# One transposed copy of the tokens, router logits as extra columns, and a gather on ScalarE, in a block of two attentions and a mixture of experts

## The chip, the cores and the metric

The kernel runs on one core of one Trainium2 chip. The metric is the device time of one execution in microseconds. A core has five engines that work beside each other, each with its own in-order queue: TensorE (PE in the profile, its weight loads are PEld), VectorE (DVE), ScalarE (ACT), GpSimd (POOL) and SyncE (SP), whose queue issues most of the DMAs. An engine that has to wait for another one waits on a semaphore, and everything behind that instruction in its queue waits with it. TensorE writes into PSUM, eight banks of 2 KB per partition; here they form two pools of four, `pu` (called by `bank_u`) and `pw` (`bank_w`).

## The reference

Everything is float32. The input `x` has 32 sequences of 256 positions with 128 features. What is computed, cut to what matters:

```
xn  = (x - mean) / sqrt(var + 1e-5)                     # over the 128 features
out = x + attn(xn) + ffn(xn)

attn(x):  q, k, v = x@Wq, x@Wk, x@Wv                    # 16 heads of 8, over the 256 positions
          scores = centred q . centred k / 8 + var(q) var(k) / 8
          return softmax(scores) @ v @ Wo

ffn(x):   hn  = layernorm(x, ln1_w, ln1_b)
          qkv = hn @ in_proj_w.T + in_proj_b            # causal attention over the first axis, 16 heads of 8:
          x1  = x + attention(qkv) @ out_proj_w.T + out_proj_b     # the 32 sequences at one position
          hn2 = layernorm(x1, ln2_w, ln2_b)
          logits = hn2 @ router_w.T                     # 8 experts, the best 2 of their softmax
          y = sum over the 2 of gate * gelu(hn2 @ w1[e]) @ w2[e]
          return x1 + y
```

So there are two attentions over the same normalised input. The one in `ffn` runs along the first axis: its "sequence" is the 32 sequences at one of the 256 positions.

## The kernel before

The 8192 tokens are handled twice, in two orders.

**The first stage** is the attention of `ffn`. It works in 16 chunks of 16 positions x 32 sequences, which makes 512 tokens, or 4 tiles of 128. `first_rounds` is a software pipeline written out by hand: iteration `i` takes chunk `i+5` from memory (`load`), measures chunk `i+4` (`measure`, by `stats`: mean and variance on DVE, the powers on POOL), normalises chunk `i+3` on ACT (`norms`), transposes and projects chunk `i+2` (`turn_in`, `project_in`), makes the scores of chunk `i+1` (`scores`, then `lessened`, which takes the row maximum off, on DVE, and `exponents` on ACT), applies the weights of chunk `i` (`turn_weights`, `weigh`, `divide`) and closes chunk `i-1` (`turn_out`, `project_out`, `normalise`). Two more steps belong to chunk `i-2`: `turn_normed` and `logits`. The order of the calls in the loop of `first_rounds` (L465 to L527) is the order in which instructions stand in each engine's queue.

For each chunk `turn_in` (L303) makes two transposed forms. One is of the normalised tokens, kept for the second stage in `xnT` (L305). The other is of the tokens normalised a second time (`zn`, L295); ScalarE applies `ln1_w` and `ln1_b` to it while it copies it out as `hT` (L310). `project_in` (L313) multiplies `hT` by the three projections: `pk` (L316), copied out by ACT in four masked forms `kb` (L320, four instructions), `pq` (L322), copied out as `qT` (L324), and `pv` (L327), copied out as `v` (L328). `v` goes to memory and back in another arrangement (`vald`, `spread`). `project_out` (L419) makes `px` (L424), adds the tokens on DVE (L426) and measures the sum; `normalise` (L433) writes the second layernorm without weights on POOL into `zx` (L436); `turn_normed` (L440) transposes that and applies `ln2_w`, `ln2_b` (L442); `logits` (L445) multiplies it by the router (L448) and DVE copies the result to `lg` (L449).

**The second stage** is the other attention, the routing and the experts. It counts in steps `t` of two heads (`step`, L942); four even values of `t` make one unit `u`, one half of the heads of a sequence, and there are 64 units. Each step has the score matmuls `sm` (L610) and `sT` (L616), the maxima on DVE (L622) and the exponentials on ACT (L625). In a step with `x == 2` comes `project` (L555): one matmul over 128 tokens of one sequence, whose stationary operand is `xnT` read with a stride of 32 elements (L557), then a square (L563) and a copy (L565) on ACT; `project_rest` (L568) copies the values out, one half on ACT (L573), one on DVE (L576). In `x == 4` comes `turn_qk` (L578), whose `pqk` is copied out by ACT (L589, L591) and DVE (L592). The steps `t = -14 .. -2` run beside what is left of the first stage (`last_rounds`).

From `t = 0` on, `route` (L717) is mixed in, some calls per step (`some`, L992: four per unit up to `t = 96`, then eight). It picks the two experts of each token, counts places, writes places and gates to memory and reads them in the order of the sequences (L792 to L798), and scatters the tokens by 128 indirect DMAs of POOL (L801). At `t = 256` the experts run as one block, and then the other 32 units with the gathers of the experts' results.

Of the kernel before, what the change touches and what calls it, by code (L numbers as in the profile page):

```python
# [19 lines left out]
P = 128  # L20
# [48 lines left out]
def block_kernel(  # L69
# [26 lines left out]
    xv = x.rearrange("s (i c k) e -> i c s (k e)", c=4, k=4)  # L96
# [7 lines left out]
    xnT = cp.tile([P, NCHUNK, 512], F32, name="xnT")  # L104
# [14 lines left out]
    rv = resd.rearrange("s (i c k) e -> i c s (k e)", c=4, k=4)  # L119

    vec = cp.tile([P, 7], F32, name="vec")
    l1w, l1b, l2w, l2b = (vec[:, n:n + 1] for n in range(4))
# [5 lines left out]
    mhalf = cp.tile([P, 4, 1], F32, name="mhalf")  # L128
    wqkv = cp.tile([P, 3, P], F32, name="wqkv")
    wo = cp.tile([P, P], F32, name="wo")  # L130
    inT = cp.tile([P, 3, P], F32, name="inT")
    outT = cp.tile([P, P], F32, name="outT")
    rT = cp.tile([P, NE], F32, name="rT")

# [5 lines left out]
    def load(i):  # L140
        xt = ax.tile([P, 4, P], F32, tag="xt", name=f"xt{i}")
        for c in range(4):
            nc.sync.dma_start(xt[32 * c:32 * c + 32].rearrange("s k e -> s (k e)"), xv[i, c])
        return xt
# [13 lines left out]
    late = xnT[:, NCHUNK - 2:NCHUNK].rearrange("p i t -> p (i t)").rearrange("p (n m) -> p n m", m=P)  # L158
    ipw, opw, qkw, rw, bvs = late[:, 0:3], late[:, 3], late[:, 4:6], late[0:NE, 6], late[:, 7]
    qkT, ccen = zx[:, NTILE - 2:NTILE], zx[:, NTILE - 3]  # L160

    def loads():

        xts[0] = load(0)
        for n, v in enumerate((ln1_w, ln1_b, ln2_w, ln2_b)):
            nc.scalar.dma_start(vec[:, n:n + 1], v.rearrange("(p o) -> p o", o=1))
        nc.scalar.dma_start(vec[:, 4:7], in_proj_b.rearrange("(t p) -> p t", p=P))
        nc.sync.dma_start(cst, consts[:, 0:C_CEN])
        nc.sync.dma_start(ipw, in_proj_w.rearrange("(t p) e -> p t e", p=P))
        nc.scalar.dma_start(opw, out_proj_w)  # L170
        nc.scalar.dma_start(bout, out_proj_b.partition_broadcast(P))
        xts[1] = load(1)
        nc.sync.dma_start(qkw[:, 0, :], Wq)
        nc.sync.dma_start(qkw[:, 1, :], Wk)
        nc.sync.dma_start(rw, router_w)
        xts[2] = load(2)
        nc.sync.dma_start(ccen, consts[:, C_CEN:C_ALL])
        nc.sync.dma_start(wqkv[:, 2, :], Wv)
        nc.sync.dma_start(wo, Wo)

    def set_in():
        nc.vector.tensor_scalar(bk4, cst[:, C_M4:C_M4 + 4], bk, None, ALU.mult)
        pt = bank_u([P, 4, P], "pt0")
        for n in range(3):
            nc.tensor.transpose(pt[:, n, :], ipw[:, n, :], ident)
        nc.tensor.transpose(pt[:, 3, :], opw, ident)
        nc.vector.tensor_copy(inT[:, 0:2, :], pt[:, 0:2, :])

        nc.vector.tensor_copy(
            inT[:, 2, :].rearrange("p (j g d) -> p j g d", j=4, g=4),  # L190
            pt[:, 2, :].rearrange("p (g j d) -> p j g d", j=4, g=4),
        )
        nc.vector.tensor_copy(outT, pt[:, 3, :])


        nc.vector.tensor_copy(bvs, bv.to_broadcast([P, P]))
        pbo = bank_u([P, P], "pbo")
        nc.tensor.matmul(pbo, bvs, outT, start=True, stop=True)
        nc.vector.tensor_tensor(bout, bout, pbo, ALU.add)

    def set_rest():
        pt = bank_w([P, 4, P], "pt1")
        nc.tensor.transpose(pt[:, 0, :], qkw[:, 0, :], ident)
        nc.tensor.transpose(pt[:, 1, :], qkw[:, 1, :], ident)
        nc.tensor.transpose(pt[:, 2, 0:NE], rw, ident[0:NE, 0:NE])
        nc.vector.tensor_copy(qkT, pt[:, 0:2, :])
        nc.vector.tensor_copy(rT, pt[:, 2, 0:NE])
        pb = bank_w([P, 2, P], "pqkw")
        for n in range(2):
            nc.tensor.matmul(pb[:, n, :], qkT[:, n, :], ccen, start=True, stop=True)  # L210
        nc.vector.tensor_copy(wqkv[:, 0:2, :], pb)

# [29 lines left out]

    def set_values(n):
        nc.gpsimd.memset(vs[n].rearrange("p j k g d -> p (j k g) d")[:, :, HD:HD + 1], 1.0)
        nc.gpsimd.memset(vbs[n], 0.0)
# [9 lines left out]
    xts, rss, nrm, mvs, zns, hTs, qTs, kbt, scs, prs, pTs, wps, os, oTs, x1s, h2s = ({} for _ in range(16))  # L255

    def stats(src, tag, i, bufs=2):

        st = a2.tile([P, 4, 6], F32, tag="st", name=f"st{tag}{i}")
        mv = a2.tile([P, 4, 2], F32, tag=f"mv{tag}", name=f"mv{tag}{i}")  # L260
# [3 lines left out]
        rs = a2.tile([P, 4, 1], F32, tag=f"rs{tag}", name=f"rs{tag}{i}")  # L264
# [4 lines left out]
    def measure(i):  # L269
# [10 lines left out]
        nc.gpsimd.tensor_tensor(r2, r2, mhalf, ALU.pow)  # L280
        nrm[i] = rs, nb, r2

# [20 lines left out]
    def turn_in(i):  # L303

        nc.scalar.copy(  # L305
            xnT[:, i, :].rearrange("p (c k s) -> p k c s", c=4, k=4),
            transposed(tokens(i), "a", i).rearrange("p (k c s) -> p k c s", k=4, c=4),
        )
        hTs[i] = a2.tile([P, 512], F32, tag="hT", name=f"hT{i}")
        nc.scalar.activation(hTs[i], transposed(zns.pop(i), "b", i), AF.Identity, bias=l1b, scale=l1w)  # L310
        nc.gpsimd.tensor_tensor(tokens(i), tokens(i), bout.unsqueeze(1).to_broadcast([P, 4, P]), ALU.add)

    def project_in(i):  # L313
        hT = hTs.pop(i)
        pk = bank_w([P, 512], f"pk{i}")
        nc.tensor.matmul(pk, inT[:, 1, :], hT, start=True, stop=True)  # L316
# [5 lines left out]
        nc.tensor.matmul(pq, inT[:, 0, :], hT, start=True, stop=True)  # L322
        qTs[i] = a2.tile([P, 512], F32, tag="qT", name=f"qT{i}")
        nc.scalar.activation(qTs[i], pq, AF.Identity, bias=bq, scale=1.0)  # L324
        pv = bank_u([P, 4, 4, 32], f"pv{i}")
        for k in range(4):
            nc.tensor.matmul(pv[:, :, k, :], hT[:, k * P:(k + 1) * P], inT[:, 2, :], start=True, stop=True)  # L327
        nc.scalar.copy(  # L328
            vs[i % 2].rearrange("p j k g d -> p (j k g) d")[:, :, 0:HD],
            pv.rearrange("p j k (g d) -> p (j k g) d", d=HD),  # L330
        )
        nc.sync.dma_start(vald[i], vs[i % 2].rearrange("p j k g d -> p j (k g d)"))
# [86 lines left out]
    def project_out(i):  # L419

        oT = oTs.pop(i)
        px = bank_w([P, 4, P], f"px{i}")
        for k in range(4):
            nc.tensor.matmul(px[:, k, :], oT[:, k * P:(k + 1) * P], outT, start=True, stop=True)  # L424
        x1 = x1s[i] = a2.tile([P, 4, P], F32, tag="x1", name=f"x1{i}")
        nc.vector.tensor_tensor(x1, px, tokens(i), ALU.add)  # L426
# [3 lines left out]
        for c in range(4):  # L430
            nc.sync.dma_start(rv[i, c], xt[32 * c:32 * c + 32].rearrange("s k e -> s (k e)"))

    def normalise(i, eng=nc.gpsimd):  # L433
        x1, mv, rs = x1s.pop(i), mvs.pop(i), rss.pop(i)
        for k in range(4):
# [4 lines left out]
    def turn_normed(i):  # L440
        h2s[i] = a2.tile([P, 512], F32, tag="h2", name=f"h2{i}")
        nc.scalar.activation(h2s[i], transposed(tokens(i), "c", i), AF.Identity, bias=l2b, scale=l2w)  # L442

    def logits(i):
        pl = bank_u([P, 4, NE], f"pl{i}")  # L445
        h2 = h2s.pop(i)
        for k in range(4):
            nc.tensor.matmul(pl[:, k, :], h2[:, k * P:(k + 1) * P], rT, start=True, stop=True)  # L448
        nc.vector.tensor_copy(lg[:, 4 * i:4 * i + 4, :], pl)  # L449
# [4 lines left out]
    def first_rounds():  # L454
# [7 lines left out]
        measure(1)  # L462
        set_values(0)
        for i in range(-2, NCHUNK):
# [23 lines left out]
            if i == NCHUNK - 1:  # L488
                project(0, 0)
                project_rest(0, 0)  # L490
# [5 lines left out]
            if i == -2:  # L496
                set_rest()
                set_values(1)
                nc.gpsimd.memset(zero, 0.0)
            if 3 <= i < 3 + NV:  # L500
                set_second(i - 3)
            if chunk(i + 3):
                norms(i + 3)
            if chunk(i + 4):
# [4 lines left out]
            if chunk(i - 1):  # L509
                normalise(i - 1)  # L510
            if chunk(i + 1):
                scores(i + 1)
            if chunk(i - 2):
                turn_normed(i - 2)
# [10 lines left out]
            if chunk(i - 2):  # L525
                logits(i - 2)

    def last_rounds():
# [5 lines left out]
        yield turn_normed(n - 1)  # L534
        yield project_out(n)
        yield logits(n - 1)
        yield normalise(n, nc.vector)
        yield turn_normed(n)
        yield logits(n)
# [5 lines left out]
    xs_all = xnT.rearrange("p i (b s) -> p (i b) s", s=NB)  # L545
    NU = 2 * NB
    pps = {}
    ot, qas, kas, exs, pos, oas, res = {}, {}, {}, {}, {}, {}, {}
# [5 lines left out]
    def project(s, ti):  # L554
# [3 lines left out]
            pp.rearrange("p n m -> p (n m)"), xs_all[:, ti * P:(ti + 1) * P, s],  # L558
# [4 lines left out]
        nc.scalar.activation(sq, pqk, AF.Square, scale=1.0 / math.sqrt(HD - 1))  # L563
        qk = qkts[s % NQ][:, ti].rearrange("p n g m r -> p (n g m) r")
        nc.scalar.copy(qk[:, :, 0:HD], pqk)  # L565
        pps[s, ti] = pp, sq

    def project_rest(s, ti):  # L568
# [4 lines left out]
        nc.scalar.copy(vo[:, :, 0, 0:8], pi[:, :, 0])  # L573
        qk = qkts[s % NQ][:, ti].rearrange("p n g m r -> p (n g m) r")
        nc.vector.tensor_reduce(qk[:, :, HD:HD + 1], sq, AX.X, ALU.add)
        nc.vector.tensor_copy(vo[:, :, 1, 8:16], pi[:, :, 1])  # L576
# [140 lines left out]
    def route():  # L717
# [3 lines left out]
        oh1, oh2 = r_tile("oh1", NTILE, NE), r_tile("oh2", NTILE, NE)  # L721
        yield nc.vector.tensor_reduce(m, lg, AX.X, ALU.max)
# [69 lines left out]
        for name, dram, src, dt in (("posb", posd, posi, I32), ("gateb", gated, gates, F32)):  # L792
            dv = dram.rearrange("s (i c k) u -> c s i (k u)", c=4, k=4)
            for c in range(4):
                nc.sync.dma_start(dv[c], src[32 * c:32 * c + 32].rearrange("p (i k) u -> p i (k u)", k=4))
# [146 lines left out]
    def step(t):  # L942
# [21 lines left out]
        if x == 6 and 0 <= u < NU:  # L964
            weigh_head(u, 0)
# [55 lines left out]
```

## Time and profile before

| what | value |
|---|---|
| median of 3 runs | 989.93 us (988.33 to 993.07) |
| the profiled execution, its own time | 992.8 us |
| its span in the trace | 991.0 us |
| mean granted TensorE clock | 0.976 |
| busy over the span | PE 940.2, DVE 706.3, ACT 655.1, POOL 561.9 us |

By stretch, busy microseconds of each engine:

| stretch, us | what runs | length | PE | DVE | ACT | POOL | clock |
|---|---|---|---|---|---|---|---|
| 0 to 60 | start, first chunks | 60 | 40.47 | 24.98 | 35.62 | 30.98 | 0.91 |
| 60 to 280 | the chunks | 220 | 197.62 | 151.12 | 158.63 | 153.74 | 0.93 |
| 280 to 300 | into the second stage | 20 | 17.63 | 17.78 | 9.08 | 2.35 | 0.83 |
| 300 to 565 | 32 units, routing, scatter | 265 | 265.00 | 231.33 | 179.96 | 124.38 | 1.00 |
| 565 to 715 | experts | 150 | 148.20 | 65.82 | 89.15 | 48.24 | 1.00 |
| 715 to 991 | 32 units, gathers, results | 276 | 271.30 | 215.29 | 182.71 | 202.23 | 1.00 |

Busy time of matmuls is modelled and they are pipelined, so a PE that is "busy" all the time need not be at its peak. The first instruction of the routing (L722) starts at 290.65 us; the first matmul of the experts that reads scattered tokens starts at 569.82 us.

### The profile page before, as it was taken

To read this page: it belongs to the slowest core of one execution; us is meant where nothing else is said; L and a number is where in the kernel's file an instruction comes from. 1 tells how busy PE (TensorE), PEld (TensorE's weight loads), DVE (VectorE), ACT (ScalarE), POOL (GpSimd) and SP (SyncE) were. 2 spreads that over 40 slices of the span, in tenths; PEclk is the share of its full clock that TensorE was granted. 3 is DMA by queue.
4 is the path that set the end of the run, shared out by engine and by line. 5 is a ranking of instruction groups with operands and counts; after the bars stand their busy time and mean duration, and the time that the engine had idled before them with its cause. 6 is when DMAs were issued, how large, how long until landed. Compare 5 with 4: busy or idle time off the path is not lost.

```text
span 991.0 us, 32300 instructions
## 1 busy us (share of the span) xinstructions
PE 940.2 (95%) x13107; PEld 679.0 (69%) x13107; DVE 706.3 (71%) x1638; ACT 655.1 (66%) x1362; POOL 561.9 (57%) x725
## 2 busy tenths in 40 slices
PE   4788999989789999999999999999999999999998
PEld 2567777777666666666666689999866666666664
DVE  2477578667589999888888834444588888888882
ACT  4687878877446666666666665555666666676664
POOL 5468787785310002777777123333387888888870
PEclk9798999999889999999999999999999999999999
DMA  3344434422031000541111134444222321121220
GB/s 100 108 132 125 134 120 139 140 60 68 21 102 35 2 2 15 59 111 55 55 53 54 52 117 135 133 134 136 76 60 63 81 69 36 39 68 52 55 60 22
DMA packets 87747, 76.32 MB, mean 77 GB/s; under 512 B 32840, under 2 KB 70864, under 8 KB 87600
## 3 DMA queue, kind: packets, MB, share of 16 engines
q1 hardware_dynamic: 74736, 48.03, 17.4%
q0 software_dynamic: 11600, 26.10, 8.5%
q8 instruction: 103, 1.69, 0.7%
q10 hardware_dynamic: 1264, 0.14, 0.1%
q14 instruction: 44, 0.36, 0.1%
HBM read 33.98 MB, written 40.24 MB: 75 GB/s over the span
## 4 chain that ended last, share of the span: by engine, by line
PE 86%; DVE 7%; issue 2%; POOL 2%; ACT 1%; DMA 0%; ACTq 0%; DVEq 0%; SPq 0%; POOLq 0%
PE sm L610 26%; PE pav L634 13%; PE pe L854 6%; PE pp L557 6%; PE ph L845 6%; PE pqk L584 3%; PE ptp L300 2%; PE sT L616 2%; PE pt L653 2%; PE sc L359 2%; DVE pr L375 2%; PE px L834 2%; PE pk L316 2%; PE px L424 2%; PE py L687 2%
## 5 line engine op out<-in xcount | busy, mean ns | idle before, releaser
L625 ACT ACTIVATE ex<-sT 128x512 f32<-128x512 f32 x512 | 277.7, 595 | 179.0 <-PE sT L616 179.0
L622 DVE TENSOR_REDUCE mt<-sm 128x2 f32<-128x512 f32 x512 | 329.0, 686 | 73.6 <-PE sT L616 67.7
L610 PE MATMUL sm<-ka,qa 32*128 32x256 f32 x2048 | 292.4, 402 | 3.5 <-DVE mt L622 3.5
L616 PE MATMUL sT<-qa,ka 32*128 32x256 f32 x2048 | 291.0, 400 | 0.0
L610 PEld LDWEIGHTS sm<-ka,qa 32*128 32x128 f32 x2048 | 177.4, 185 | 81.0 <-issue 38.1
L616 PEld LDWEIGHTS sT<-qa,ka 32*128 32x128 f32 x2048 | 176.4, 184 | 2.6 <-issue 1.7
L801 POOL DMA_INDIRECT xsd<-zx,posi x128 | 122.9, 960 | 81.4 <-DVE posi L789 42.7
L905 POOL DMA_INDIRECT yg<-ysd,posb x128 | 122.1, 954 | 43.0 <-issue 31.5
L634 PE MATMUL pav<-ex,va 128*32 128x256 f32 x2048 | 137.2, 385 | 0.0
L859 POOL DMA_DIRECT2D ysd<-ye x71 | 48.2, 679 | 115.0 <-DVE ye L858 89.1
L634 PEld LDWEIGHTS pav<-ex,va 128*32 128x32 f32 x2048 | 53.8, 109 | 64.2 <-issue 24.0
L854 PEld LDWEIGHTS pe<-w,ge 128*128 128x128 f32 x568 | 74.5, 192 | 4.2 <-ACT ge L847 0.7
L854 PE MATMUL pe<-w,ge 128*128 128x128 f32 x568 | 74.9, 275 | 0.3 <-ACT ge L847 0.3
L845 PE MATMUL ph<-xT,w 128*128 128x256 f32 x284 | 73.3, 381 | 0.0
L557 PE MATMUL pp<-wqkv,xnT 128*128 128x384 f32 x128 | 65.6, 595 | 0.8 <-DVE mt L622 0.8
L858 DVE COPY ye<-pe 128x256 f32<-128x256 f32 x71 | 30.1, 424 | 50.8 <-PE pe L854 50.8
L837 ACT ACTIVATE xT<-px,vec 128x256 f32<-128x256 f32 x71 | 39.9, 563 | 35.8 <-PE px L834 35.8
L847 ACT ACTIVATE ge<-ph 128x512 f32<-128x512 f32 x71 | 42.4, 597 | 21.1 <-PE ph L845 21.1
L378 ACT ACTIVATE pr<-pr 128x1024 f32<-128x1024 f32 x32 | 33.8, 1058 | 34.0 <-DVE pr L375 33.9
L374 DVE TENSOR_REDUCE mx<-sc 128x16 f32<-128x512 f32 x64 | 43.4, 678 | 17.3 <-PE sc L359 17.3
L828 DVE COPY w<-wall 128x512 f32 x71 | 30.4, 429 | 33.3 <-issue 31.9
L845 PEld LDWEIGHTS ph<-xT,w 128*128 128x128 f32 x284 | 48.5, 191 | 4.1 <-ACT xT L837 0.4
(170 smaller groups left out, 1663.0 us busy)
## 6 DMA issues: line engine op xcount, KB each, us to landing
xb<-xsd SPq DMA_DIRECT2D x71, 128.0 KB, 2.1
ysd<-ye POOLq DMA_DIRECT2D x71, 128.0 KB
xsd<-zero SPq DMA_DIRECT2D x10, 852.0 KB
vald<-v SPq DMA_DIRECT2D x16, 288.0 KB, 2.3
vb<-vald SPq DMA_DIRECT2D x64, 72.0 KB, 3.0
xt<-in_L_attn_x_dram SPq DMA_DIRECT2D x64, 64.0 KB, 2.0
resd<-xt SPq DMA_DIRECT2D x64, 64.0 KB, 1.7
res<-resd SPq DMA_DIRECT2D x32, 128.0 KB, 3.3
```

Source lines behind the costliest of these rows:

```text
L374: nc.vector.tensor_reduce(mx, s, AX.X, ALU.max)
L557: nc.tensor.matmul(pp.rearrange("p n m -> p (n m)"), xs_all[:, ti * P:(ti + 1) * P, s], wqkv.rearrange("p n m -> p (n m)"), start=True, st ...
L610: nc.tensor.matmul(sc[:, i, :], qas[u][r:r + 32, i * P:(i + 1) * P], kas[u][r:r + 32, h, :], start=True, stop=True,)
L616: nc.tensor.matmul(sc[:, i, :], kas[u][r:r + 32, h, i * P:(i + 1) * P], qas[u][r:r + 32, :], start=True, stop=True,)
L622: nc.vector.tensor_reduce(mts[y // 8 % 2][:, :, o:o + 1], sc, AX.X, ALU.max, negate=True)
L625: nc.scalar.activation(exs[y], sc, AF.Exp, scale=1.0 / HD)
L634: nc.tensor.matmul(pos[u][32 * j:32 * j + 32, :], vaugs[s % NV][:, ti, 4 * j + 2 * g + h, :], exs[8 * u + 4 * h + j][:, ti, :], start=(h = ...
L801: yield nc.gpsimd.indirect_dma_start(xsd_views[n * NTILE + k], bass.IndirectOffsetOnAxis(ap=posi[:, k, n:n + 1], axis=0), zx[:, k, :], None,)
L845: nc.tensor.matmul(ph[:, f, :], wb[n][0][:, f * P:(f + 1) * P], xT, start=True, stop=True)
L854: nc.tensor.matmul(pe[:, j, :], ge[:, f, j * P:(j + 1) * P], w2b[:, f, :], start=(f == 0), stop=(f == 1))
L859: nc.gpsimd.dma_start(ysd[n * BLK:(n + 1) * BLK].rearrange("(p j) h -> p j h", j=2), ye)
L905: yield nc.gpsimd.indirect_dma_start(yg[s][:, ti, n, :], None, ysd, bass.IndirectOffsetOnAxis(ap=gt["posb"][:, s, ti, n:n + 1], axis=0),)
```

## The change

What it does, part by part:

- **One transposed form.** `turn_in` transposes only `zn`; the copy goes to `znT`, which takes the place of `xnT` and is kept for the second stage. `ln1_w` is folded into the projections (`inT`, `inV`), `ln1_b` into their biases (`set_in`). The order of tokens in a chunk changes from (c, k) to (k, c), so that the rows of `x` are read, and those of `resd` written, in pieces of 128 elements and no longer of 512.
- **The second stage reads `znT`**, which was scaled a second time, and takes that scaling back: `invert` keeps the reciprocals in `rall`, `scale_back` brings them through memory into the order of the sequences (`rpos`), and `project` and `project_rest` multiply by them. `gather` copies the 256 columns of one sequence out of `znT` into a contiguous tile on ScalarE; `project` reads that.
- **Extra columns for the logits.** `turn_normed` and `logits` are gone. The logits are built from the values' matmul, which has 160 columns instead of 128 and is made in two halves, and from the output's matmul, 136 columns instead of 128, also in halves; a multiplication, two additions and, in `route`, five POOL instructions over 64 x 8 elements put them together.
- **Filling and measuring moved.** `measure(1)` stands between the weights' copies in `set_in`; `set_values(1)` and the zero tile are filled one iteration later. Of the four instructions of `normalise`, two move from POOL to DVE.

```diff
-    xv = x.rearrange("s (i c k) e -> i c s (k e)", c=4, k=4)
+    xv = x.rearrange("s (i k c) e -> i c s k e", c=4, k=4)
...
     def set_in():
-        nc.vector.tensor_scalar(bk4, cst[:, C_M4:C_M4 + 4], bk, None, ALU.mult)
...
-        nc.vector.tensor_copy(inT[:, 0:2, :], pt[:, 0:2, :])
...
+        nc.tensor.transpose(pr, rw, ident[0:NE, 0:NE])
+        nc.vector.tensor_scalar(inT, pt[:, 0:2, :], l1w, None, ALU.mult)
+        measure(1)
+
+        nc.vector.memset(inV[:, 4, :], 0.0)
+        nc.vector.tensor_scalar(
+            inV[:, 0:4, :].rearrange("p j (g d) -> p j g d", g=4),
             pt[:, 2, :].rearrange("p (g j d) -> p j g d", j=4, g=4),
+            l1w, None, ALU.mult,
         )
+        nc.vector.tensor_copy(rT, pr)
+        nc.vector.tensor_scalar(rP, rT, l2w, None, ALU.mult)
+        nc.vector.tensor_tensor(ipb, ipw, l1bs.unsqueeze(1).to_broadcast([P, 3, P]), ALU.mult)
+        nc.vector.tensor_reduce(bz, ipb, AX.X, ALU.add)
+        nc.vector.tensor_tensor(vec[:, 4:7], vec[:, 4:7], bz.rearrange("p n o -> p (n o)"), ALU.add)
+        nc.vector.tensor_scalar(bk4, cst[:, C_M4:C_M4 + 4], bk, None, ALU.mult)
         nc.vector.tensor_copy(outT, pt[:, 3, :])
...
+    def invert(i):
+
+        nc.vector.reciprocal(rall[:, 4 * i:4 * i + 4], r2s.pop(i).rearrange("p k o -> p (k o)"))
...
     def turn_in(i):
-
-        nc.scalar.copy(
-            xnT[:, i, :].rearrange("p (c k s) -> p k c s", c=4, k=4),
-            transposed(tokens(i), "a", i).rearrange("p (k c s) -> p k c s", k=4, c=4),
-        )
-        hTs[i] = a2.tile([P, 512], F32, tag="hT", name=f"hT{i}")
-        nc.scalar.activation(hTs[i], transposed(zns.pop(i), "b", i), AF.Identity, bias=l1b, scale=l1w)
+        nc.scalar.copy(znT[:, i, :], transposed(zns.pop(i), "b", i))
         nc.gpsimd.tensor_tensor(tokens(i), tokens(i), bout.unsqueeze(1).to_broadcast([P, 4, P]), ALU.add)
...
-        pv = bank_u([P, 4, 4, 32], f"pv{i}")
-        for k in range(4):
-            nc.tensor.matmul(pv[:, :, k, :], hT[:, k * P:(k + 1) * P], inT[:, 2, :], start=True, stop=True)
-        nc.scalar.copy(
-            vs[i % 2].rearrange("p j k g d -> p (j k g) d")[:, :, 0:HD],
-            pv.rearrange("p j k (g d) -> p (j k g) d", d=HD),
-        )
-        nc.sync.dma_start(vald[i], vs[i % 2].rearrange("p j k g d -> p j (k g d)"))
+
+        v = vs[i % 2]
+        for h in range(2):
+            pv = bank_u([P, 5, 2, 32], f"pv{i}_{h}")
+            for k in range(2):
+                o = (2 * h + k) * P
+                nc.tensor.matmul(pv[:, :, k, :], zT[:, o:o + P], inV, start=True, stop=True)
+            nc.scalar.copy(
+                v[:, :, 2 * h:2 * h + 2].rearrange("p j k g d -> p j (k g) d")[:, :, :, 0:HD],
+                pv[:, 0:4].rearrange("p j k (g d) -> p j (k g) d", d=HD),
+            )
+            t = slice(4 * i + 2 * h, 4 * i + 2 * h + 2)
+            nc.vector.tensor_tensor(
+                lg[:, t, :], pv[:, 4, :, 0:NE], rall[:, t].unsqueeze(2).to_broadcast([P, 2, NE]), ALU.mult
+            )
+        nc.sync.dma_start(vald[i], v.rearrange("p j k g d -> p j (k g d)"))
...
     def project_out(i):
...
-        nc.vector.tensor_tensor(x1, px, tokens(i), ALU.add)
+        for h in range(2):
+            px = bank_w([P, 2, P + NE], f"px{i}_{h}")
+            for k in range(2):
+                o = (2 * h + k) * P
+                nc.tensor.matmul(px[:, k, :], oT[:, o:o + P], outX, start=True, stop=True)
+            nc.vector.tensor_tensor(
+                x1[:, 2 * h:2 * h + 2, :], px[:, :, 0:P], tokens(i)[:, 2 * h:2 * h + 2, :], ALU.add
+            )
+            l = lg[:, 4 * i + 2 * h:4 * i + 2 * h + 2, :]
+            nc.vector.tensor_tensor(l, l, px[:, :, P:P + NE], ALU.add)
...
-    def turn_normed(i):
-        h2s[i] = a2.tile([P, 512], F32, tag="h2", name=f"h2{i}")
-        nc.scalar.activation(h2s[i], transposed(tokens(i), "c", i), AF.Identity, bias=l2b, scale=l2w)
-
-    def logits(i):
-        pl = bank_u([P, 4, NE], f"pl{i}")
-        h2 = h2s.pop(i)
-        for k in range(4):
-            nc.tensor.matmul(pl[:, k, :], h2[:, k * P:(k + 1) * P], rT, start=True, stop=True)
-        nc.vector.tensor_copy(lg[:, 4 * i:4 * i + 4, :], pl)
+    def scale_back():
+
+        pr = bank_u([NTILE, P], "pra")
+        nc.tensor.transpose(pr, rall, ident)
+        ra = a1.tile([NTILE, P], F32, tag="ra", name="ra")
+        nc.vector.tensor_copy(ra, pr)
+        nc.sync.dma_start(rnd.rearrange("(n c) s -> n (c s)", c=4), ra)
+        nc.sync.dma_start(rpos[:, 0], rnd.rearrange("(i t) s -> t i s", t=P))
+        nc.vector.tensor_scalar(rpos[:, 1], rpos[:, 0], 1.0 / math.sqrt(HD - 1), None, ALU.mult)
...
+            if chunk(i + 3):
+                invert(i + 3)
             if chunk(i + 4):
                 measure(i + 4)
...
             if chunk(i - 1):
-                normalise(i - 1)
+                normalise(i - 1, nc.gpsimd, (0, 1))
...
-            if chunk(i - 2):
-                logits(i - 2)
+            if chunk(i - 1):
+                normalise(i - 1, nc.vector, (2, 3))
+            if i == NCHUNK - 3:
+                scale_back()
...
+    def gather(s):
+
+        xs[s] = bh.tile([P, SEQ], F32, tag="xs", name=f"xs{s}", bufs=2)
+        nc.scalar.copy(xs[s], xs_all[:, :, s])
...
-            pp.rearrange("p n m -> p (n m)"), xs_all[:, ti * P:(ti + 1) * P, s],
+            pp.rearrange("p n m -> p (n m)"), xs[s][:, ti * P:(ti + 1) * P],
...
-        nc.scalar.activation(sq, pqk, AF.Square, scale=1.0 / math.sqrt(HD - 1))
+        nc.scalar.activation(sq, pqk, AF.Square, scale=rpos[:, 1, ti, s:s + 1])
...
-        nc.scalar.copy(qk[:, :, 0:HD], pqk)
+        nc.scalar.activation(qk[:, :, 0:HD], pqk, AF.Identity, scale=rpos[:, 0, ti, s:s + 1])
...
+        yield nc.gpsimd.tensor_tensor(
+            t, mvall[:, :, 0:1].to_broadcast(all8), rows[:, 1:2, :].to_broadcast(all8), ALU.mult
+        )
+        yield nc.gpsimd.tensor_tensor(lg, lg, t, ALU.subtract)
...
-            dv = dram.rearrange("s (i c k) u -> c s i (k u)", c=4, k=4)
+            dv = dram.rearrange("s (n c) u -> c s n u", c=4)
...
+        if x == 6:
+            if 0 <= u < NU:
+                weigh_head(u, 0)
+            if u % 2 == 0 and 2 <= u // 2 + 3 < NB:
+                gather(u // 2 + 3)
```

In the queues of the changed program the multiplication that writes `lg` in `project_in` stands on DVE after the fourth `lessened` of its iteration and ahead of the additions of `project_out`, and its semaphore counts ScalarE's copy of the same half of `pv`.

## The prediction

> **What bounds the kernel now.** I read the page first, then busy time by stretch, then the waits of the first stage, the chain of waits in each stage, and the order of time over one chunk.
>
> From 300 us to the end TensorE decides. In the chain of waits over two thirds of a unit (start, length, what) it is never released by another engine:
>
> ```profile
> 441.38 0.20 PE sm L610 x2
> 441.58 0.01 PE sT L616 x2
> 441.60 0.20 PE sm L610 x2
> 441.80 0.01 PE sT L616 x2
> 441.81 0.95 PE pp L557 x2
> 442.76 0.22 PE po L679 x2
> ```
>
> So there a shorter `pp` is worth something, and work on other engines only where it makes TensorE wait. The first stage is different. The waits from 40 to 265 us (total, times, longest):
>
> ```profile
> DVE x L426 <- PE px L424: 46.6, 14, 4.6
> ...
> ACT pr L378 <- DVE pr L375: 31.5, 26, 2.0
> ```
>
> VectorE waits once in each chunk, in front of L426, and ScalarE waits for VectorE: the two and TensorE form a ring. In order of time, one turn of it, of both windows the lines of ScalarE and VectorE that close it:
>
> ```profile
> 193.33 0.69 DVE L426 TENSOR_TENSOR x<-px,zx 128x512 f32<-128x512 f32 x1 [3.25 <-PE px L424]
> ...
> 203.69 0.69 DVE L375 TENSOR_TENSOR pr<-sc,mx 128x512 f32<-128x512 f32 x1
> ...
> 204.48 1.06 ACT L378 ACTIVATE pr<-pr 128x1024 f32<-128x1024 f32 x1 [1.02 <-DVE pr L375]
> ```
> ```profile
> 205.44 0.57 ACT L417 COPY oT<-pto 128x512 f32<-128x512 f32 x1
> ...
> 205.91 2.79 ACT L320 ACTIVATE kb<-pk,bk,cst 128x512 f32<-128x512 f32 x4
> ...
> 207.33 0.69 DVE L426 TENSOR_TENSOR x<-px,zx 128x512 f32<-128x512 f32 x1 [2.94 <-PE px L424]
> ...
> 208.57 0.71 ACT L324 ACTIVATE qT<-pq,vec 128x512 f32<-128x512 f32 x1
> ...
> 209.14 0.61 ACT L328 COPY v<-pv 128x512 f32<-128x512 f32 x1
> ```
>
> From L426 to L426 are 14.00 us. By the starts of the instructions the turn consists of: wait for `px` 2.95, L426 0.73, the statistics of two tiles 3.29, two `lessened` 2.69, a `divide` 0.72, the logits' copy L449 0.10, `lessened` 1.40, `divide` 0.72, `lessened` 1.40, together 14.00. Over twelve turns (L426 starts at 57.41 and at 236.62) the mean is 14.93: some turns are held up by POOL's fillings or a slow TensorE clock. The reader is to see that VectorE resumes at 207.33, while ScalarE finishes `v` only near 209.75.
>
> **The change, part by part** (the sum is on the profiled span, 991.0).
>
> *The new wait, in each chunk.* `project_in` now puts two multiplications (`lg` from `pv` and `rall`) on VectorE, ahead of the additions that take the place of L426. They read the tile that ScalarE copies `v` out of, and wait for that copy. Does such a wait hold VectorE up? The trace has the same pair, L591 and L592, which read one `pqk`:
>
> ```profile
> 286.31 1.06 PE L584 MATMUL pqk<-cst,qk 128*128 128x128 f32 x4
> ...
> 287.68 0.48 ACT L591 ACTIVATE ka<-pqk,cst 128x256 f32<-128x256 f32 x1
> ...
> 288.19 0.48 DVE L592 TENSOR_SCALAR ka<-pqk,cst 128x256 f32<-128x256 f32 x1 [1.21 <-ACT ka L591]
> ```
>
> TensorE is done at 287.37, VectorE idles, and starts when ScalarE has ended. The Trainium skill, "PSUM — Partial Sum Buffer", section "PSUM bank collisions raise a hardware error", says that no two engines may read one bank of the same partitions together and that the software has to keep them apart. It speaks against this change: the extra columns lie in the bank that another engine is to read.
>
> ScalarE comes late to that copy. Its queue after L375 at 204.38 is: L378, L417, four L320, L324, then `v`. L378 itself waits for L375, so nothing of it can be moved ahead. By starts it reaches `v` at 209.14; two halves of 256 elements at 0.39 each (L565, the same size out of PSUM: 392 ns), 0.36 apart, end at 209.89. That is 5.51 after L375's end, against 2.95 now. The new turn: 5.55 with a semaphore; second multiplication 0.10; two half additions and two additions to `lg` 0.95 (L671, 256 elements: 0.41, some 0.35 apart; small ones 0.10 apart, as L449); statistics 3.29; reciprocal 0.10; 2.69; 0.72; two `normalise` on VectorE 0.58 (four of L436 took 1.15 on it); 1.40; 0.72; 1.40. Sum 17.5. Without the wait (by the matmuls alone) it would be 2.95 + 11.85 = 14.8, as much as now. Twelve turns at 17.5 against 14.93: **+30.8**. POOL's fillings and TensorE's instruction stalls (1.69 at 212.03) now lie under the wait. What is behind the waiting multiplication on VectorE: L426's successors, both statistics, `lessened`; for these wait ScalarE's exponentials and through them TensorE's `ptp`.
>
> *What is taken off.* Per chunk on TensorE `pta` 0.44, `ptc` 0.44, `pl` 0.95, against 0.2 for wider `pv` and 0.05 for wider `px`; on ScalarE L305 0.57 and L442 0.80; on POOL two L436, 1.59. None of these is on the ring, so they bring nothing in the twelve turns. In the drain after the last `project_in` TensorE is on the chain for about half the time: five chunks' `ptc` and `pl` are 7 us, half of it saved, less 2 for VectorE's additions: **-2**.
>
> *Start.* `measure(1)` (1.65) and seven small instructions now precede `outT` and `bvs` (L196, 1.02), and TensorE's `pbo` stands ahead of the first `ptb`: VectorE gets there near 16.5 and not 12.5, `ptb` comes 3.1 later, `pta` no longer between. Chunk 1 gains the filling of L245 (1.92 on the chain at 19.35) but ScalarE's `norms(1)` waits for chunk 0's `v`. Net +2.3 at the first `lessened`; iterations 0 and 1 add 0.95 and 2.75 by the same wait: **+6**.
>
> *`scale_back`.* Its last instruction on VectorE waits for two DMAs in a row, with `lessened` behind it. By the nearest rows (resd to landing 1.7, res 3.3, issues 0.4 each) and a transposition and copy before: **+5.5**; VectorE has nothing to hide it.
>
> *Second stage.* The stationary operand becomes contiguous: L557's weight load is 304 ns, L854's of the same size 192. It is exposed: `pp` takes 0.95 on the chain for 768 columns, `pk` 0.86 for 1024, at whose rate 768 are 0.645, and the rest is 0.305. Gain 0.11 for each of 64: 7.2. Against it ScalarE's scale by a pointer: L591 493 ns against L589 379 for the same copy, so L563 and L565 +0.11 each and L573 +0.07. The second copy of values on VectorE (L576) waits for L573, and the maxima (L622) behind it free the bank of an `sm` with some 0.2 to spare: 0.29 later leaves TensorE waiting 0.08. The gather (0.39, half as often) fits into idle time before L625 (0.44 to 0.99). Between full gain and a loss of as much I take **-2**. The routing starts five calls later. Its first scatter comes a unit later (8.7), of 14.5 us between the landing of the first `xb` (555.3) and its use (569.82), so hidden. The places are written in pieces of 8 bytes instead of 32, four times the packets, and the fetches of `res` behind them in SP's queue come some 14 later; the seventh is used at 434.5 and landed at 421.3. **+1**, between 0 and 6.
>
> *TensorE's clock.* After a stall of 1.69 the trace shows eight `ptp` at 1.90 instead of 0.87. The skill, "TensorE: Matmul & The Clock Gate", Part 1, says that an idle window of about 3.4 us halves the clock for as long. The new turn leaves TensorE idle for about 5 us before `ptp`. By the row such a dip costs some 0.3 a turn, since `pk` has 1.5 to spare before L320; by the rule at its worst, with the scores slow too, 3. I take the row: **+3**, worst +36.
>
> Sum: 30.8 + 6 - 2 + 5.5 - 2 + 1 + 3 = +42, span 1033; the median lay 1.1 below the span: **1032**.
>
> **Rivals.** *The wait is not there* (VectorE needs only the matmul): turn 14.8, 12 x 0.1 less, start +3 only, so 991 - 1 + 3 - 2 + 5.5 - 2 + 1 = 995. For it: two reads change nothing of each other. Against: the 1.21 above, and the semaphore in the changed queues, which counts ScalarE's copy. *TensorE decides the first stage*, faster: it is 90% busy from 60 to 280 (197.62 of 220), and 1.6 off each of 12 turns, 4 in the drain and the full 7.2 give 991 - 30 = 960. It decides only if `v` ends before `px`, 2.95 after L375; ScalarE's queue says 5.5. *The clock drops for whole turns*: +3 more for 11 turns, 1066. For it: the stretch 80 to 100 had 0.83 with far shorter gaps; against: TensorE has 6 us to spare.
>
> **Chances.** Forecast 0.74 (1012 to 1050); wait absent 0.07; TensorE decides 0.05; clock 0.14. The range 1006 to 1058 leaves out the faster cases and the worst of the clock. Two runs differ by some 0.5%, so within 5 us counts as no change: faster 0.06, same 0.04, slower 0.90.
>
> **What would show it.** L426's successor idles some 5.5 us behind the first multiplication, waiting for `v`; turns of 17.5; TensorE near 65% busy in the first stage; VectorE idle about 5 after `scale_back`; `pp`'s weight load near 190 ns; units at 8.5 to 8.7. If turns are near 15, the wait is not as I read it; if the units grow, ScalarE's scaling is the cause.

## The result: 1084.5 us, over twice the loss that was forecast

| | before | after |
|---|---|---|
| median | 991.5 us (4 runs, 988.33 to 993.39) | 1084.52 us (4 runs, 1081.56 to 1085.82) |
| span of the profiled execution | 991.0 | 1079.8 |
| mean granted TensorE clock | 0.976 | 0.937 |

The ratio is 1.0937, with a 95% interval of 1.0896 to 1.0979. The forecast was 1032 (1006 to 1058), so the direction was right and the size wrong by 52 us.

To find where the time went I compared starts of the same instructions in both traces: the first additions to `px` of chunks 0 and 12 (L426 before, L474 after), and the fourth, seventeenth and twenty-third `pp` of the second stage (each stands in the trace as two matmuls). The table splits the 88.8 us of the two spans; the forecast's terms stand beside it.

| stretch | before | after | difference | forecast |
|---|---|---|---|---|
| start to chunk 0's addition | 57.41 | 62.10 | +4.7 | +6 |
| twelve turns of the chunks | 179.21 | 207.42 | +28.2 | +30.8 and +3 for the clock |
| chunk 12's addition to 4th `pp` | 46.97 | 56.16 | +9.2 | -2 and +5.5 |
| 4th to 17th `pp` (routing runs beside) | 115.00 | 118.53 | +3.5 | nothing |
| 17th to 23rd `pp` | 51.65 | 97.47 | **+45.8** | **+1** |
| 23rd `pp` to the end | 540.76 | 538.12 | -2.6 | -2 |

The first stage is near the forecast. The waits of the changed kernel from 40 to 330 us (total, times, longest), and the multiplication's group in the page's costliest groups (busy and mean; idle time ahead of it and who ended it):

```profile
ACT pr L424 <- DVE pr L421: 84.1, 27, 7.0
...
DVE lg L375 <- ACT v L370: 73.9, 14, 5.7
...
PEld ptp L344 <- ACT qT L362: 19.3, 14, 1.8
```
```profile
L375 DVE TENSOR_TENSOR lg<-pv,rall 128x16 f32<-128x16 f32 x32 | 5.6, 175 | 87.4 <-ACT v L370 85.9
```

The wait for `px` is all but gone (3.4 us in two waits) and a longer one, for ScalarE's copy of `v`, has its place. One closing of the ring in order of time (start, length; idle time ahead in brackets):

```profile
218.29 0.71 ACT L362 ACTIVATE qT<-pq,vec 128x512 f32<-128x512 f32 x1
218.86 0.67 ACT L370 COPY v<-pv 128x256 f32<-128x256 f32 x2
...
219.29 0.45 DVE L375 TENSOR_TENSOR lg<-pv,rall 128x16 f32<-128x16 f32 x2 [5.46 <-ACT v L370]
219.66 0.41 DVE L474 TENSOR_TENSOR x<-px,zx 128x256 f32<-128x256 f32 x1
```

VectorE idles 5.46 us and starts once the first half of `v` is copied. The undisturbed turn is 16.98 us and the mean 17.28.

What the forecast missed stands in the chain of waits of the changed kernel, from 446 to 527 us:

```profile
446.14 0.70 DVE mt L682
447.02 0.94 SPq L863
448.00 3.81 SPq L863
451.85 26.24 DMA posd<-posi
478.16 0.37 SPq L866
478.57 2.83 SPq L866
481.45 3.35 SPq L863
484.84 2.59 SPq L863
487.49 3.81 SPq L863
491.35 23.02 DMA gated<-gates
514.46 0.36 SPq L866
514.82 0.35 issue
515.17 3.01 SPq L866
518.24 5.74 DMA res<-resd
524.07 0.42 DVE res L748
```

Read it as a story of one queue. SP issues the writes of the places; the reads behind them wait until the writes have landed, 26 us later; then come the gates, another 23; and only then does SP reach the fetch of the residual for which VectorE waits. In the kernel before, the same chain from 395 to 432 us lies on TensorE without a break. The waits of the changed kernel from 400 to 620 us name the damage:

```profile
DVE res L748 <- DMA res<-resd: 36.4, 1, 36.4
PE sm L670 <- DVE va L636: 35.4, 1, 35.4
```

One VectorE instruction waits 36.4 us, the copy of the next values (L636) stands behind it in the queue, and TensorE waits for that. The clock falls with it: in the stretch from 500 to 510 us TensorE does nothing and 0.50 is granted.

### The profile page after: what moved, and what is told of

Read it like the earlier page. It is cut to its first block, busy times and chain, and to the rows that moved or that the text cites. A ratio compares the mean times of both kernels' runs of the same rounds, so it can differ in the third digit from the quotient of the medians.

```text
span 1079.8 us, 31869 instructions
## 1 busy us (share of the span) xinstructions
PE 934.2 (87%) x12861; PEld 657.5 (61%) x12861; DVE 728.1 (67%) x1759; ACT 668.7 (62%) x1378; POOL 545.1 (50%) x700
## 3 DMA queue, kind: packets, MB, share of 16 engines
q1 hardware_dynamic: 99648, 48.09, 19.3%
## 4 chain that ended last, share of the span: by engine, by line
PE 65%; DVE 15%; ACT 7%; DMA 7%; issue 3%; SPq 2%; POOL 1%; DVEq 0%; ACTq 0%; POOLq 0%
PE sm L670 22%; PE pav L694 11%; PE pe L922 6%; PE ph L913 6%; PE pp L616 4%; ACT kb L358 4%; DVE pr L421 3%; DVE mx L420 3%; DMA posd<-posi 2%; PE pqk L644 2%; PE sT L676 2%; DMA gated<-gates 2%; PE pt L713 2%; PE px L902 1%; SPq L863 1%
## 5 line engine op out<-in xcount | busy, mean ns | idle before, releaser
L670 PE MATMUL sm<-ka,qa 32*128 32x256 f32 x2048 | 302.3, 407 | 39.3 <-DVE va L636 35.4
L676 PE MATMUL sT<-qa,ka 32*128 32x256 f32 x2048 | 295.7, 405 | 2.1 <-issue 2.1
L670 PEld LDWEIGHTS sm<-ka,qa 32*128 32x128 f32 x2048 | 185.2, 187 | 120.6 <-issue 63.2
L676 PEld LDWEIGHTS sT<-qa,ka 32*128 32x128 f32 x2048 | 179.8, 187 | 5.1 <-issue 4.2
L344 PE MATMUL ptp<-cst,pr 128*128 128x128 f32 x256 | 49.3, 344 | 22.8 <-ACT qT L362 15.8
L304 POOL TENSOR_SCALAR rsall<-mvall 128x4 f32<-128x4 f32 x16 | 3.7, 232 | 127.8 <-DVE rall L325 81.3
L616 PE MATMUL pp<-wqkv,xs 128*128 128x384 f32 x128 | 60.5, 556 | 5.4 <-ACT xs L607 2.8
L375 DVE TENSOR_TENSOR lg<-pv,rall 128x16 f32<-128x16 f32 x32 | 5.6, 175 | 87.4 <-ACT v L370 85.9
```

The lines of the kernel that those rows point to most:

```text
L344: nc.tensor.transpose(pt[:, k, :], src[:, k, :], ident)
L616: nc.tensor.matmul(pp.rearrange("p n m -> p (n m)"), xs[s][:, ti * P:(ti + 1) * P], wqkv.rearrange("p n m -> p (n m)"), start=True, stop=True,
L670: nc.tensor.matmul(sc[:, i, :], qas[u][r:r + 32, i * P:(i + 1) * P], kas[u][r:r + 32, h, :], start=True, stop=True,)
L676: nc.tensor.matmul(sc[:, i, :], kas[u][r:r + 32, h, i * P:(i + 1) * P], qas[u][r:r + 32, :], start=True, stop=True,)
```

## The experiments

Runs of the kernel before on the same chips gave medians of 991.5 to 992.2.

**swap: VectorE reads the bank first.**

```diff
+            t = slice(4 * i + 2 * h, 4 * i + 2 * h + 2)
+            nc.vector.tensor_tensor(lg[:, t, :], pv[:, 4, :, 0:NE], ..., ALU.mult)
             nc.scalar.copy(v[...], pv[:, 0:4]...)
-            t = slice(4 * i + 2 * h, 4 * i + 2 * h + 2)
-            nc.vector.tensor_tensor(lg[:, t, :], pv[:, 4, :, 0:NE], ..., ALU.mult)
```

> The changed kernel, with the multiplication of each half of the logits written ahead of ScalarE's copy of the same PSUM tile, so that VectorE reads it first and needs only the matmuls. Theory (the wait for ScalarE's copy stretches the ring): the 5.2 to 5.7 us of idle time ahead of the multiplication shrink to what the matmuls need, turns of the first stage fall from 17.28 to about 14.9, 12 x 2.4 = 29 us less: 1056 from 1084.5. Rival (the additional columns and VectorE's longer list hold the ring anyway): turns stay near 17, time within 5 us of 1084.5. If TensorE's slow clock in the drain comes from the ring's idle time, the 18.4 us that the drain has grown by shrink too, and the time is nearer to 1040.

Measured: 1060.67 us (1.0709 of before, 1.0659 to 1.0760), 24 less than the changed kernel. The wait for `v` is not in the trace any more; the turn fell from 17.28 to 15.62. That shows the wait, set by the order of the two readers, as the cause of most of the longer turn, but 15.62 is not 14.9. The waits of this kernel from 60 to 245 us:

```profile
DVE lg L371 <- PE pv L369: 29.4, 24, 3.3
...
PE ptp L344 <- ACT qT L362: 12.2, 11, 1.6
DVE mx L420 <- PE sc L405: 11.6, 9, 3.0
```

VectorE now waits for the matmuls. The second line is new to the analysis: TensorE's `ptp` waits for ScalarE's `qT`, though it does not read it. The drain (the end of the first stage, chunk 12's addition to the fourth `pp`) did not shrink: 59.4, after 56.2. So the idea that its slow TensorE comes from the ring's idle time got no support. (The 18.4 us of the expectation are not this stretch, which had grown by 9.2.)

**posd: large pieces for places and gates.**

```diff
-    posd = dp.tile([NB, SEQ, 2], I32, name="posd")
+    posd = dp.tile([4, NB, NTILE, 2], I32, name="posd")
...
-            dv = dram.rearrange("s (n c) u -> c s n u", c=4)
             for c in range(4):
-                nc.sync.dma_start(dv[c], src[32 * c:32 * c + 32])
+                nc.sync.dma_start(dram[c], src[32 * c:32 * c + 32])
...
-                nc.sync.dma_start(dst[:, :, ti, :], dram[:, ti * P:(ti + 1) * P, :].rearrange("s t u -> t s u"))
+                nc.sync.dma_start(dst[:, :, ti, :], dram[:, :, 32 * ti:32 * ti + 32, :].rearrange("c s n u -> n c s u"))
```

> The changed kernel, with the DRAM copies of the places and gates laid out by residue, position group and tile, so that each of the eight writes has pieces of 512 bytes, where it had 8; the reads keep their pieces of 8 bytes. Theory (the small pieces fill SP's queue and the DMA engines, and the fetches of the residual behind them come late): from the first write to the first fetch of a residual some 20 us and not 72, the wait of 36.4 us for a residual is gone, 1084.5 - 37 = 1047. Rival (the reads of 8 bytes are as costly as the writes): less than half of it, about 1070. Rival (the middle is long because ScalarE scales by a pointer): no change, 1084.

Measured: 1038.83 us (1.0478, 1.0444 to 1.0513), 45.7 less. The 17th to the 23rd `pp` took 52.6 us. SP's queue (start, time, what it issues) of the changed kernel, of the kernel before and of this one, in that order:

```profile
446.33 15.35 SPq L863 DMA_DIRECT2D posd<-posi  x4
478.16 3.24 SPq L866 DMA_DIRECT2D posb<-posd  x2
481.45 16.71 SPq L863 DMA_DIRECT2D gated<-gates  x4
514.46 3.73 SPq L866 DMA_DIRECT2D gateb<-gated  x2
518.24 8.40 SPq L611 DMA_DIRECT2D res<-resd  x10
```
```profile
396.45 2.71 SPq L795 DMA_DIRECT2D posd<-posi  x4
402.63 3.23 SPq L798 DMA_DIRECT2D posb<-posd  x2
405.90 5.99 SPq L795 DMA_DIRECT2D gated<-gates  x4
414.16 3.79 SPq L798 DMA_DIRECT2D gateb<-gated  x2
418.00 8.89 SPq L552 DMA_DIRECT2D res<-resd  x10
```
```profile
447.93 1.75 SPq L862 DMA_DIRECT2D posd<-posi  x4
450.96 3.33 SPq L865 DMA_DIRECT2D posb<-posd  x2
454.33 3.81 SPq L862 DMA_DIRECT2D gated<-gates  x4
459.61 3.20 SPq L865 DMA_DIRECT2D gateb<-gated  x2
462.87 8.16 SPq L611 DMA_DIRECT2D res<-resd  x10
```

From the first write to the first fetch are 71.9, 21.6 and 14.9 us. The reads, in pieces of 8 bytes in all three, hold SP as long each time (3.2 to 3.8 us for two), and the time came back though they were left as they are; so the rival that blames them falls. The one that blames ScalarE's scaling falls too, since posd keeps it.

**b_posd8: the small pieces alone, in the kernel before.**

```diff
-            dv = dram.rearrange("s (i c k) u -> c s i (k u)", c=4, k=4)
+            dv = dram.rearrange("s (n c) u -> c s n u", c=4)
             for c in range(4):
-                nc.sync.dma_start(dv[c], src[32 * c:32 * c + 32].rearrange("p (i k) u -> p i (k u)", k=4))
+                nc.sync.dma_start(dv[c], src[32 * c:32 * c + 32])
```

> The kernel before, with one edit: the places and gates are written in pieces of 8 bytes in place of 32, as the changed kernel writes them; they are read back in an order that does not match, so the outputs of the last stage are combined from other rows (the work is the same). Theory: the small pieces alone cost the middle of the kernel 30 to 37 us: 1022 to 1028 from 991.5. The prediction's term: 0 to 6 us, 992 to 998. If it is between, the shift of the routing by the late first stage takes part of it.

Measured: 1032.88 us (1.0425, 1.0389 to 1.0461), 41 more than before; from the 17th to the 23rd `pp` pass 89.0 us in place of 51.6. The first stage is untouched, so the term needs no later start of the routing. The pages count 12288 more packets under 512 B than before, which is what eight writes of 2048 pieces in place of 512 must give.

**ahead: order in the queue, or busy DMA engines?** The fetches of the first 16 residuals are issued before the writes.

```diff
     RESIDUALS = {18 + i: [18 + i, NB - 6 + 2 * i, NB - 5 + 2 * i] for i in range(3)}
+    RESIDUALS.update({s: [] for s in range(1, 16)})
+    RESIDUALS[0] = list(range(16))
```

> The changed kernel, with the fetches of the first 16 residuals issued together, ahead of the writes of the places and gates in SP's queue; these writes keep their pieces of 8 bytes. It separates the two ways in which the small pieces can hurt. Theory (order in the queue: the fetches stand behind writes whose issue takes 15 to 17 us for four): no wait for a residual, the 36 us go though the writes are as slow as ever: 1040 to 1050. Rival (the packets hold the DMA engines, so that everything moved at that time is late, the scatter and the rows of the feed-forward part too): 1075 or more. Between: both take part.

Measured: 1051.43 us (1.0612, 1.0575 to 1.0650), 33 less than the changed kernel, with writes nearly as slow as before (those of the gates 16.53 us):

```profile
448.68 14.02 SPq L863 DMA_DIRECT2D posd<-posi  x4
```

No instruction waits for a residual, and the 17th to the 23rd `pp` take 59.8 us in place of 97.5. So about 38 of the 45.8 us are order in the queue. Only 33 of them reach the median, and the rival has a part: behind the 23rd `pp` this trace loses 4.4 us, 3.4 of them around the experts' block. POOL's scatter, with the time for which it waited for its own earlier DMAs, in this kernel and in posd, shows how:

```profile
L869 POOL DMA_INDIRECT xsd<-zx,posi x128: 952/958/1242, 446.1 to 622.1; - x128
...
  DMA xsd<-zx,posi: 19.0, 12
```
```profile
L868 POOL DMA_INDIRECT xsd<-zx,posi x128: 954/958/1242, 445.4 to 606.0; - x128
...
  DMA xsd<-zx,posi: 0.3, 1
```

With the small packets moving, the scatter's issues spread over 176.0 us and not 160.6. The experts' first matmul comes at 626.5, 4.4 us behind the last issue; in posd it comes at 617.2, with 11.2 us between them, so there the scatter had time to spare and here it has not. The other 7 to 8 us lie in the stretch to the 23rd `pp` itself; what lengthens it there is not shown, and I leave it open.

**all3: both edits, and the end of `scale_back` on GpSimd.** The third edit, in `scale_back`:

```diff
-        nc.vector.tensor_scalar(rpos[:, 1], rpos[:, 0], 1.0 / math.sqrt(HD - 1), None, ALU.mult)
+        nc.gpsimd.tensor_scalar(rpos[:, 1], rpos[:, 0], 1.0 / math.sqrt(HD - 1), None, ALU.mult)
```

> Both edits together, and the last multiplication of scale_back on GpSimd, so that VectorE does not wait for its two DMAs. If the parts add: 1084.5 - 29 - 37 - 5 = 1013. If the drain's slow clock is a consequence of the ring's idle time: 1000 or less. If one of them only uncovers another limit: over 1025.

Measured: 1014.06 us (1.0230, 1.0198 to 1.0263). The sum is met, but with some luck: swap and posd gave 23.9 and 45.7 where 29 and 37 were summed, which alone makes 1015; of the 6.0 by which the third edit shortens the drain against swap, 3.2 only undo what it had grown there. In swap, in order of time on VectorE, this multiplication had cost

```profile
263.83 0.20 DVE L500 TENSOR_SCALAR rpos<-rpos 128x64 f32<-128x64 f32 x1 [4.98 <-DMA rpos<-rnd]
```

and chunk 12's addition to the fourth `pp` now takes 53.4 instead of 59.4. The turns are still 15.60.

**banks: `pv` takes one place of the rotation again.** `pu` has four buffers, handed out in turn. Before, `pq`, one `pv` and two `ptp` followed each other; with two halves of `pv` the second `ptp` gets the buffer of `pq`, and must wait until ScalarE has copied `qT` out of it.

```diff
-            pv = bank_u([P, 5, 2, 32], f"pv{i}_{h}")
+            pv = (bank_u if h else bank_w)([P, 5, 2, 32], f"pv{i}_{h}")
```

> The kernel with the three edits together (1014.1), and the first half of `pv` in the other group of four PSUM buffers (that of `pk` and `px`). In that kernel the turns are still 15.60, against 14.93 before: TensorE's second transposed tile of weights waits 1.6 us in each turn for ScalarE's `qT`, because two half tiles of `pv` take two places in the rotation where one stood, and the scores and VectorE's maxima behind it come late. Theory: this wait goes, turns near 14.9, 12 x 0.7 = 8 us less: 1006. Rival (the ring is held by TensorE's `pv` and `px` at a lower clock): within 3 us of 1014.

Measured: 1004.85 us (1.0150, 1.0102 to 1.0197), 9 less. The wait of `ptp` for `qT` is no longer among the waits from 60 to 240 us, and VectorE's wait for the scores is halved:

```profile
DVE mx L420 <- PE sc L405: 5.8, 9, 2.1
```

The turn is 15.23, so 4.4 of the 9 us lie in the twelve turns. This execution also reached chunk 0's addition at 56.93 and not 62.46; how much of that is the edit is open, since three kernels that do not differ up to there (the changed one, posd and ahead) reach it at 62.1, 64.1 and 65.0.

**best: gathering early, multiplications of chunks 0 to 2 put off.** On top of banks, the first two `gather` calls move from ahead of `project(0, 0)` in the last iteration to the end of `exponents` in the one before, and `project_in` of the first three chunks leaves its multiplications to a call behind `measure(i + 4)`.

> The kernel of the edit before (half of `pv` in the other buffers), and two more: the first two gatherings stand one iteration earlier, where ScalarE is idle, and not between the last oT and the first `pp`; the multiplications of the logits of chunks 0 to 2 stand behind the statistics, since these chunks have no px to wait for. Theory: TensorE's 2.8 us in front of the first `pp` go, and some 3 us of the start (the waits of iterations 0 and 1): 5 less than the kernel without them, 1001. If the repaired change beats the kernel before, it is under 987; by the stages of the traces (routing +3.4, the rest of the drain) it should not.

Measured: 1005.73 us (1.0142, 1.0102 to 1.0182), no gain. In the profiled execution the stretch to the fourth `pp` fell from 52.5 to 47.9 us, but chunk 0's addition came at 61.65 and not 56.93. The second reading is not firm, since the start of one and the same code differs by up to 3 us between executions. So I took the second edit out again:

**early: the gathering alone.**

> The kernel with half of `pv` in the other buffers (1004.9), and of the two edits that came out even together only the earlier gathering of the first two sequences. By the starts of the instructions that gathering gave 4.6 us between the additions of chunk 12 and the fourth `pp` (52.5 to 47.9), and the multiplications put off in the first chunks cost 4.7 before the first addition. Theory: 1000. Rival (the two are not independent, or the start differs between executions): 1003 to 1006. Under 987, and so ahead of the kernel before, it should not be.

Measured: 1006.31 us (1.0146, 1.0114 to 1.0177; five runs from 1001.28 to 1009.02), the same as banks within its spread. The stretch to the fourth `pp` was 49.4, in place of 52.5. This is inconclusive: a gain of some 3 us in one trace is smaller than the spread of the times.

**b_gather: the gathering in the kernel before.** Only `gather`, its calls (the first two early) and the contiguous operand:

```diff
-            pp.rearrange("p n m -> p (n m)"), xs_all[:, ti * P:(ti + 1) * P, s],
+            pp.rearrange("p n m -> p (n m)"), xs[s][:, ti * P:(ti + 1) * P],
```

> The kernel before with the gathering alone: ScalarE copies the 256 columns of a sequence to a contiguous tile, which `pp` takes as its stationary operand (the first two an iteration early). Theory: `pp` falls by what two units show in the changed kernel, 17.06 against 17.2, 0.08 for each of 64 calls: 5 less, 986. By the weight load's rows (304 against 192 ns) 7 less, 984.5. Rival (ScalarE's copies come in the way of the exponentials): no gain, or slower.

Measured: 986.16 us (18 runs), against 991.53 (21 runs) for the kernel before: 0.9947, 0.9931 to 0.9964. The gain is small but clear of the spread, and it is the fastest kernel of this study. `pp` in the view of one tile from 300 to 900 us (duration min/median/max in ns), before and here:

```profile
L557 PEld LDWEIGHTS pp<-wqkv,xnT x106: 291/304/319, 301.4 to 895.1; 128*128 128x128 f32 x106
L557 PE MATMUL pp<-wqkv,xnT x106: 485/591/698, 301.4 to 895.4; 128*128 128x384 f32 x106
```
```profile
L565 PEld LDWEIGHTS pp<-wqkv,xs x108: 186/188/189, 301.8 to 899.4; 128*128 128x128 f32 x108
L565 PE MATMUL pp<-wqkv,xs x108: 486/538/590, 301.8 to 899.7; 128*128 128x384 f32 x108
```

The weight load costs 188 ns and no longer 304. From the 23rd to the 35th `pp` pass 102.0 us against 103.3 before: 0.105 less for each unit, as the rows of the weight loads said.

## Why the prediction was right and where it failed

- **The new wait** was right in place, size and mechanism: 5.1 to 5.7 us in every chunk but the first (6.9), where 5.5 was worked out; undisturbed turns of 16.98, 17.28 in the mean, where 17.5 was. The swap showed that it is the order of the two readers, not the additional work. What the step did not see is the second effect of the halves, the place in the rotation of buffers. It hid under the long wait (19.3 us of TensorE's weight loads waited for `qT` in the changed kernel too) and showed only when that was gone; so the 14.8 without the wait was too low, 15.6 was measured. The sum also set turns without disturbances, 17.5 and 14.8, against the mean of 14.93, though the undisturbed turn before was 14.00: "as much as now" was a gain of nothing only by that mixture.
- **The start** was right within its spread: +4.7 for +6. Three traces with the old start reach chunk 0's addition at 57.4, 58.5 and 59.4, three with the new one at 62.1, 64.1 and 65.0.
- **`scale_back`** was right: 4.88 us idle in the changed kernel, 6.0 less in the stretch when it left VectorE. **What is taken off** in the drain was not: the stretch grew 9.2 where 3.5 was summed. Some 3 to 5 of it may lie in the first two gatherings, which stand between ScalarE's last `oT` and the first `pp` (TensorE idles 2.78 us ahead of it, until the first of them is done); the timed runs are too coarse to confirm that. The granted clock in this stretch was 0.86 before and 0.76 after; whether it is a cause or follows the waits is open.
- **The second stage** was right from the 23rd `pp` on: -2.6 for -2. That is in part luck: the figure was a middle between a gain of 7.2 and as much loss, and where the routing runs beside it, from the 4th to the 17th `pp`, 3.5 us were lost that no term had. All traces of the changed kernel and its repairs keep them (118.0 to 119.2 in place of 115.0); the cause is open. The full gain of the contiguous operand is 0.105 for each unit (b_gather), 0.08 of it is left beside ScalarE's scalings. These took 0.08 to 0.09 us more for each instruction, near the 0.07 and 0.11 expected, but by the difference of the two kernels TensorE lost 0.03 and not 0.08. A gathering took 637 ns and not 390, without harm that the units show.
- **The failed step** is the sentence "the fetches of `res` behind them in SP's queue come some 14 later; the seventh is used at 434.5 and landed at 421.3. +1, between 0 and 6." The mechanism was seen and the term mis-sized: the way from the first write to the first fetch grew from 21.6 to 71.9 us, 50 and not 14, against a slack of 13.2. It measured +45.8, with +41 for the same edit alone in the kernel before. The issues of the eight writes alone grew by 23.4 (15.35 and 16.71 against 2.71 and 5.99), and the waits of the reads for the landings, twice in a row, by the other 27.0 (16.5 and 16.3 against 3.5 and 2.3). The prediction shows no working for its 14. With the term gone, in posd, the time was 1038.8, seven above the forecast. That closeness is in part luck: a first stage forecast 6.9 too long stands against a drain and a routing forecast 9.2 too short.
- **The clock.** The mean fell from 0.976 to 0.937, but part of this is the stall at 490 to 525 us. In the twelve turns it was 0.94 before, 0.88 with the new wait and 0.94 again in swap, so here it followed the idle time; TensorE was busy 76% of the turns, where 65% was expected. Whether the turns hold the +3 cannot be told, and no run tried the clock by itself; the turns leave no room for the worst of +36.
- **The rivals.** "The wait is not there" is refuted by the trace. "TensorE decides the first stage" is refuted too: even without the wait and with the rotation mended the turn is 15.23, not under 14.93. "The clock drops for whole turns" gives a time nearer to the measured one, but for a reason that the trace does not show.

## What to carry to other kernels

When a layout change makes a DMA's pieces smaller, price the whole chain in its queue: issue, landing, what waits for the landing, and what stands behind all this in the same queue; compare the sum with the slack of the first consumer. When two engines read one PSUM tile, let the reader whose queue is waited for go first; and when a tile is split in two, count the places in the rotation of buffers. A mixed change is best tried in parts: here its gather alone makes the kernel 0.5% faster, while the whole makes it 9.4% slower.

## What I had not expected of the hardware

Four writes of together 64 KB took, from the first issue to the start of the read that waits for them, 3.03 us (places) and 5.28 us (gates) in pieces of 512 bytes, 6.18 and 8.26 in pieces of 32, and 31.83 and 33.01 in pieces of 8, each time with the scatter beside them. Four times the packets cost four to five times the time, and SP itself was held 15.35 and 16.71 us by the four issues, where it was held 2.71 and 5.99 (32 bytes) and 1.75 and 3.81 (512). The Trainium skill, "DMA: Bandwidth & Descriptors", section "Specifications", gives 512 bytes as the least transfer for the full rate, with a read-modify-write below it. The direction agrees, but the step from 512 to 32 cost only 3 us here and the step from 32 to 8 another 25 to 26; no run here shows whether a read-modify-write is what costs it.
